# Layer 2 of a four-layer convolution kernel: raw v instead of a normalised copy, output statistics as sums on ScalarE, taps shared anew, and three pieces of work placed elsewhere

## The chip, the cores and the metric

The kernel runs on one core of a Trainium2 chip. The metric is the device time of one execution in microseconds (us); the time of a kernel is the median of its runs. Engines are named as the profile names them: PE is TensorE (PEld its weight loads), DVE is VectorE, ACT is ScalarE, POOL is GpSimd, and SP is the engine whose queue issues most transfers.

## The reference

Eight images of 128 channels and 96 x 96 points, in float32, go through four layers. Each adds to its input a convolution of its group normalisation (32 groups of four channels):

```
for layer in (L0, L1, L2, L3):
    x = x + conv_layer(group_norm_32(x))

L0: deformable 3x3 convolution (DCNv4): depthwise 3x3, layer norm, gelu, then
    offsets and masks per point, bilinear samples, weighted sum
L1: dense 3x3 convolution, 128 -> 128 channels
L2: q  = sign(x);  xq = (q - tanh(alpha_x * x)) + tanh(alpha_x * x)
    wq = the same of weight and alpha_w
    out = dwconv3x3(xq, weight) + dwconv3x3(x, wq)
L3: row by row over H: row h adds to row h+1 a relu of a 9-tap convolution along W, with bias
```

In L2 the `x` of the formulas is already normalised: x = sc * v + bi, where v is the output of layer 1 and sc, bi are one number per image and channel.

## The kernel before

The 128 channels are the 128 partitions. The kernel has three stages.

*Layer 0* ends at about 3472 us of the span. Its samples are taken as weighted sums over 25 shifts, which holds while no offset exceeds 1. Each chunk adds what exceeds 1 into a column of `beyond`; after the last chunk these are reduced to one number, `flag`, which all engines read (`values_load`, then `tc.If`) to choose between the fast way and a fallback.

*Layers 1 and 2* are one stage, from 3477 to 4828 us; its tiles have names that end in C. An image is cut into 12 chunks of 8 rows (`NCH` = 12, `CR` = 8).

- `conv_chunk(i, c)` does layer 1 for one chunk: it loads y with one row more on either side (`yw`), normalises it on ACT (L1252), forms four combinations `d` on POOL (L1259), multiplies them on PE with weights of 128 x 128 (L1272), and adds the four products on DVE into `vn` (L1288, L1296, L1308). `bn_stats` on DVE (L1317) collects the statistics of v. Two whole images of v are kept, `vns[i % 2]`, each with a border of one point.
- `v_coefs(i)` turns the statistics of an image into `sc_v`, `bi_v` (bn_aggr, two small PE products with a matrix of group means, one square root on ACT).
- An ACT pass (L1546), one operation for each chunk, then overwrites v with its normalised value. The border stays zero.
- `tap_chunk(i, c)` does layer 2 for one chunk. ACT makes sign and tanh (`sg` L1355, `th` L1357), POOL makes of them `xq` (L1362, L1368). There are 17 taps and a centre: eight of v with weights `wsg`, nine of `xq` with weights `w2s`. The centre of v is an ACT operation into PSUM (L1444). A tap can go one of three ways. POOL's way: ACT makes a scaled copy `pt` (L1414) and POOL adds such copies up (L1423). PE's way: eight products with diagonal matrices of 64 x 64 (`dgv` for v, `dgx` for xq, L1385), which PE adds up in PSUM. DVE's way: one multiply-and-add on PSUM (L1406). PE then merges the sums of POOL and of DVE (after a copy `ac` on ACT, L1458) into its own (L1392). ACT evicts the result to `o` (L1467), SP stores it, and two `bn_stats` on DVE (L1480) take the statistics of the output.
- `out_coefs(i)` turns these into `sc3`, `bi3`, the scale and offset of layer 3.

How many taps go which way is in two tables, `TAPS1` for images 0 to 6 and `TAPS2` for the last one: pairs (POOL, PE) for chunk 0, 1, 2, 3, then again; DVE has the rest of the 17.

Taps run `LAG` = 14 chunks behind the convolution, so that image i's convolution runs beside image i-1's taps. Each engine executes in the order in which the instructions were written. That order comes from the class `Plan`: every piece of work is a `task` with an engine, an assumed cost, what it depends on, a priority and the buffers that it uses. `Plan.order` walks through time with these costs and gives each free engine the ready task of lowest priority number whose buffers are free. For PE, a task of the same tile shape (64 or 128 wide) is preferred while its priority is within `KEEP` of the best. The constants at the top of the file (`PE_AT`, `DVE_AT`, `SUM_AT`, ...) shift priorities.

*Layer 3* runs from 4828 to the end; its names end in D. `load(g)` brings four rows of all eight images into `xtD` (1.5 MB), with three such groups resident. `norm(g, i)` (L1634) makes the normalised copy `xgD` on ACT. Then for each row DVE prepares (`row`, L1656 and L1658; `tr`, L1660 to L1662), PE multiplies (L1675), ACT applies the relu (L1614) and POOL adds it to the next row (L1615). Loads 0 and 1 are issued on POOL's queue after everything of layer 2; the SBUF of layer 2's tiles is taken over by layer 3's. `late_weights` prepares layer 3's weights: one load, `k3s`, and six DVE operations, `km` (L1159 to L1164), at the start of the stage of layers 1 and 2.

Of the kernel before, what the change touches and what calls it, by code (L numbers as in the profile page):

```python
# [19 lines left out]
P = 128  # L20
NG = 8
GC = P // NG
K2 = 9
# [8 lines left out]
TAPS1 = ((4, 6), (4, 5), (3, 6), (4, 6))  # L32
TAPS2 = ((3, 11), (1, 10), (5, 10))


POOL_AT, MERGE_AT = -22, 13
PE_AT, PE_PACE = 5, 5.3
DVE_AT, DVE_PACE = -57, 1.4
L1_AT, L1_PACE = -4, 0.0
SUM_AT = 2  # L40
STATS_AT = 59
KEEP12 = 14.0
# [171 lines left out]
def kernel(  # L214
# [197 lines left out]
    with ExitStack() as ph:  # L412
# [310 lines left out]
        def chunk(i, c, at, made):  # L723
# [37 lines left out]
            for k in (1, 0):  # L761
# [29 lines left out]
                plan.task(  # L791
# [5 lines left out]
                )  # L797
# [137 lines left out]
        squares = {}  # L935
        weights = conv_weights(-STEP * NST)
        made = {0: image(0, -STEP * NST)}
        for i in range(N):
            for c in range(NST):
                at = STEP * (i * NST + c)  # L940
                chunk(i, c, at, made[i])
            plan.task("DVE", 0.7, lambda i=i: y_stats(i), squares[i], at + 2 * STEP)
            if i + 1 < N:
                made[i + 1] = image(i + 1, STEP * i * NST)
        with tc.manual_schedule():
            plan.emit()


            m1 = sp.tile([P, 1], F32, name="m1")
            nc.vector.tensor_reduce(m1[:], beyond[:], AX.X, ALU.max)  # L950
            pt = plan.pools["s"].tiles[0]
            nc.tensor.transpose(pt[:1, 0, :P], m1[:], ident[:])
            m2 = sp.tile([1, 1], F32, name="m2")
            nc.vector.tensor_reduce(m2[:], pt[:1, 0, :P], AX.X, ALU.max)
            nc.vector.tensor_scalar(flag[:], m2[:], 0.0, None, ALU.is_gt)
# [137 lines left out]

    sc3 = const.tile([P, N], F32, name="sc3")
# [7 lines left out]
    with ExitStack() as ph:  # L1102
        wp = ph.enter_context(tc.tile_pool(name="wpC", bufs=1))
# [7 lines left out]
        for name, n, shape in (  # L1111
            ("yw", 3, [P, CR + 2, W + 2]), ("d", 2, [P, 4, NP1, W + 2]),
            ("sg", 2, [P, CR + 2, W]), ("th", 2, [P, CR + 2, W]), ("xq", 3, [P, CR + 2, W + 2]),
            ("ac", 2, [P, CB, FB]), ("o", 2, [P, NB, FB]), ("pt", 8, [P, CB, FB]),
        ):
            tiles = [wp.tile(shape, F32, name=f"{name}C{k}") for k in range(n)]
            if name in ("yw", "xq"):
                for t in tiles:
                    nc.gpsimd.memset(t[:, :, 0:1], 0.0)
                    nc.gpsimd.memset(t[:, :, W + 1 : W + 2], 0.0)  # L1120
            plan.pool(name, tiles)
# [8 lines left out]
        dgs = [wp.tile([P, K2, HC], F32, name=name) for name in ("dgv", "dgx")]  # L1130

        def tap_weights(at):


            def signs():
                nc.scalar.activation(wsg[:], w2s[:], AF.Sign)
                nc.scalar.activation(wth[:], w2s[:], AF.Tanh, scale=alw[:])

            def both():
                nc.vector.tensor_tensor(wsg[:], wsg[:], wth[:], ALU.subtract)  # L1140
                nc.vector.tensor_tensor(wsg[:], wsg[:], wth[:], ALU.add)

            def diagonal(dg, w, t):
                nc.vector.tensor_scalar(dg[:, t, :], idq[:], w[:, t : t + 1], None, ALU.mult)

            s = plan.task("ACT", 1.9, signs, [], at)
            s = plan.task("DVE", 0.4, both, [s], at)
            return [s] + [
                plan.task("DVE", 0.16, lambda a=(dg, w, t): diagonal(*a), [s], at)
                for dg, w in zip(dgs, (wsg, w2s)) for t in range(K2)  # L1150
            ]

        def late_weights(at):

            ld = plan.task("SP", 0.6, lambda: nc.sync.dma_start(k3s[:], k3), [], at, lag=4.0)
            v = nc.vector
            t = []
            for fn in (
# [12 lines left out]
                for name, n in (  # L1171
                    ("st2", NCH * CB * 6), ("st3", NB * NCH * 6), ("wc", 1),
                    *((f"{a}_{b}", 1) for a in ("mean", "v", "sd", "sc", "bi") for b in "yv"), ("mv_v", 2),
                    ("mv_o", 2 * NB), ("d_o", NB), ("mean_o", 1), ("sd_o", 1),
# [23 lines left out]
        def group_coefs(i, kind, mv, deps, prio):  # L1198
# [3 lines left out]

            def mid(ps):
                nc.vector.tensor_copy(mean[:], ps[:, 0, 0:1])
                add_square(v[:], ps, 0, mv[:, 0:1], mv[:, 1:2])

            b1 = plan.buf("v")
            t = plan.task(
                "PE", 0.4, lambda: nc.tensor.matmul(b1.tile[:, 0, 0:1], gmean[:], mv[:, 0:1], start=True, stop=True),
                deps, prio, uses=[b1],  # L1210
            )
# [113 lines left out]
        def v_coefs(i, stats, at):  # L1325
            s = smalls[i % 2]
            mean_y, sc, bi, sd, mv = s["mean_y"], s["sc_v"], s["bi_v"], s["sd_v"], s["mv_v"]

            def aggr():
                nc.vector.bn_aggr(mv[:], s["st2"][:])  # L1330
                nc.vector.tensor_scalar(mv[:, 0:1], mv[:, 0:1], mean_y[:], None, ALU.add)

            t = plan.task("DVE", 0.9, aggr, stats, at)
            t = group_coefs(i, "v", mv[:], [t], -1e6)

            def end():
                nc.vector.tensor_scalar(bi[:], mean_y[:], sc[:], bi[:], ALU.mult, ALU.add)

                nc.vector.tensor_scalar(s["wc"][:], sd[:], wsg[:, CENTER : CENTER + 1], None, ALU.add)

            return plan.task("DVE", 0.4, end, [t], -1e6)


        def tap_chunk(i, c, norms, at, n_pool, n_pe):
# [7 lines left out]
            near = norms[max(c - 1, 0) : c + 2]  # L1352

            readers = [
                plan.task("ACT", 1.0, lambda: nc.scalar.activation(sg.tile[:, :n, :], v, AF.Sign), near, at - 24, uses=[sg]),  # L1355
                plan.task(
                    "ACT", 1.05, lambda: nc.scalar.activation(th.tile[:, :n, :], v, AF.Tanh, scale=alx[:]), near, at - 23, uses=[th]  # L1357
# [23 lines left out]
            def tap_pe(src, t, first):  # L1381
                for j in range(NB):
                    for b in range(CB):
                        t_, rows, cols = source(src, t, b, RB)
                        nc.tensor.matmul(  # L1385
                            pq.tile[half(b), j, :FB], dgs[src][half(j), t, :], t_[half(j), rows, cols], start=first, stop=False
# [16 lines left out]
            def tap_dve(src, t):  # L1403
                w = (wsg, w2s)[src]
# [5 lines left out]
            for k, (_, t) in enumerate(all_taps[:n_pool]):  # L1410
# [4 lines left out]
                        rows_of(pt.tile[:]), rows8(0, t), AF.Identity, scale=wsg[:, t : t + 1]  # L1415
# [32 lines left out]
            for k, (src, t) in enumerate(all_taps[n_pool + n_pe :]):  # L1448
# [9 lines left out]
                lambda: nc.scalar.activation(ac.tile[:], pd.tile[:, :, :FB], AF.Identity, bias=s["mean_v"][:]),  # L1458
# [7 lines left out]
            t = plan.task(  # L1466
                "ACT", 0.82, lambda: nc.scalar.activation(o.tile[:], pq.tile[:, :, :FB], AF.Identity), [t], at + 10, uses=[pq, o]  # L1467
            )

            def store():  # L1470
# [7 lines left out]
            st = s["st3"][:].rearrange("p (j c k) -> p j c k", j=NB, k=6)  # L1478
            stats = [
                plan.task("DVE", 0.49, lambda j=j: nc.vector.bn_stats(st[:, j, c, :], o.tile[:, j, :]), [t], at + STATS_AT, uses=[o])  # L1480
                for j in range(NB)
            ]
            return readers, stats

        def out_coefs(i, stats, at):
# [3 lines left out]
            mv, d, mean, sd = s["mv_o"][:].rearrange("p (j k) -> p j k", k=2), s["d_o"], s["mean_o"], s["sd_o"]  # L1489
            st = s["st3"][:].rearrange("p (j f) -> p j f", j=NB)  # L1490

            def aggr():
                for j in range(NB):
                    nc.vector.bn_aggr(mv[:, j, :], st[:, j, :])

            def means(ps):
                nc.tensor.matmul(ps[:, 0, 0:NB], gmq[:], mv[:, :, 0], start=True, stop=True)
                for j in range(NB):
                    nc.tensor.matmul(ps[half(j), 1, 0:1], gmq[:, half(0)], mv[:, j, 0:1], start=True, stop=True)

            def mid(ps):
                nc.vector.tensor_copy(mean[:], ps[:, 1, 0:1])
                for j in range(NB):
                    add_square(d[:, j : j + 1], ps, j, mv[:, j, 0:1], mv[:, j, 1:2])
# [24 lines left out]
        weights = tap_weights(20 * 4)  # L1529
        late_weights(20 * 2 * NCH)  # L1530
        for i in range(N):
# [6 lines left out]
            done = v_coefs(i, stats + ends.get(i - 2, []) + (weights if i == 0 else []), 20 * (i + 1) * NCH)  # L1538
            made[i] = [done]
            norms = []  # L1540
            for c in range(NCH):
                s = smalls[i % 2]
                rows = inner(vns[i % 2], c * CR, (c + 1) * CR)
                norms.append(plan.task(
                    "ACT", 0.98,
                    lambda rows=rows, s=s: nc.scalar.activation(  # L1546
                        rows, rows, AF.Identity, bias=s["bi_v"][:], scale=s["sc_v"][:]
                    ),
                    [done], 20 * (i * NCH + c + LAG) - 45,
                ))  # L1550
            outs = []
            for c in range(NCH):
                taps = TAPS1 if i < N - 1 else TAPS2
                readers, st = tap_chunk(i, c, norms, 20 * (i * NCH + c + LAG), *taps[c % len(taps)])
# [11 lines left out]
    with ExitStack() as ph:  # L1566

        wp = ph.enter_context(tc.tile_pool(name="wpD", bufs=1))
        xts = [wp.tile([P, N, LG, W], F32, name=f"xtD{g}") for g in range(3)]
        xgs = [wp.tile([P, N, LG, W], F32, name=f"xgD{g}") for g in range(3)]  # L1570
# [68 lines left out]
        with tc.manual_schedule():  # L1639
            for g in range(2):  # L1640
                load(g, nc.gpsimd)
# [122 lines left out]
```

## Time and profile before

| What | us |
|---|---|
| median of three runs | 5604.98 (5604.57 to 5605.74) |
| the profiled execution, its own time | 5606.45 |
| its span in the profile | 5604.7 |
| busy: PE | 5382.2 (96% of the span) |
| busy: DVE | 4839.3 (86%) |
| busy: POOL | 4554.4 (81%) |
| busy: ACT | 3371.5 (60%) |

The granted clock is 0.99 over the span. Shares over the whole span are averages over three stages with different work. For this change the stage of layers 1 and 2, from 3477 to 4828 us, its beginning and its two ends matter; they are read by windows. An operation in the profile is named by line, engine, tile written and tile read.

### The profile page before, as it was taken

The numbers are of one execution on the slowest core, as the hardware profiler recorded it, in microseconds if no ns is written. First come the engines' busy times: TensorE is split into PE (matmuls) and PEld (weight loads), VectorE is DVE, ScalarE is ACT, GpSimd is POOL, SyncE is SP. The second block draws the span as 40 slices with busy tenths as digits, with TensorE's granted clock in tenths as the row PEclk, the third lists the DMA queues.
The fourth block names the chain that finished last, engine by engine and source line by source line (L and its number), as shares of the span: only waits on it lengthen the run. The fifth ranks groups of instructions, "written<-read, shape, count | busy, mean of one in ns | idle before, by whom it ended". The sixth has DMA issues, their size and how long they took to land. (4 is left out here: it accounts for less than half of the span.)

```text
span 5604.7 us, 128829 instructions
## 1 busy us (share of the span) xinstructions
PE 5382.2 (96%) x53049; PEld 3007.8 (54%) x53049; DVE 4839.3 (86%) x6874; ACT 3371.5 (60%) x4816; POOL 4554.4 (81%) x2835
## 2 busy tenths in 40 slices
PE   5899999999999999999999998999999999899999
PEld 2354454454454454454454443545454554699999
DVE  5788888888888888888888998699999998688887
ACT  4656666656766666666666663477787777533333
POOL 0899999999999999999999998699999998422222
PEclk9999999999999999999999999999999999999999
DMA  6121121221212112112111111222222221223232
GB/s 128 48 60 58 54 61 58 56 61 58 56 59 60 54 58 61 55 59 60 46 49 47 43 41 40 61 67 64 66 67 67 65 66 48 83 95 109 94 110 80
DMA packets 423809, 360.65 MB, mean 64 GB/s; under 512 B 251889, under 2 KB 422417, under 8 KB 423217
## 3 DMA queue, kind: packets, MB, share of 16 engines
q1 hardware_dynamic: 390336, 310.33, 19.7%
q10 hardware_dynamic: 32144, 38.87, 2.0%
q8 instruction: 422, 6.91, 0.5%
q0 software_dynamic: 736, 3.15, 0.2%
q14 instruction: 171, 1.39, 0.1%
HBM read 201.26 MB, written 150.99 MB: 63 GB/s over the span
## 5 line engine op out<-in xcount | busy, mean ns | idle before, releaser
L862 PE MATMUL ps_w<-wt,sel 64*64 64x384 f32 x19200 | 1857.1, 488 | 58.7 <-DVE h L809 17.2
L879 DVE TENSOR_TENSOR pr<-ps_w,xq 128x768 f32<-128x768 f32 x1824 | 1670.0, 949 | 209.4 <-PE ps_w L862 158.7
L852 POOL TENSOR_TENSOR wt<-h,h 128x768 f32<-128x768 f32 x864 | 1583.9, 1838 | 262.1 <-DVE h L809 140.3
L897 POOL TENSOR_TENSOR acc<-acc,pr 128x768 f32<-128x768 f32 x882 | 1618.6, 1837 | 72.4 <-DVE pr L879 60.0
L862 PEld LDWEIGHTS ps_w<-wt,sel 64*64 64x64 f32 x19200 | 743.9, 133 | 925.3 <-issue 287.7
L1272 PE MATMUL pv_C<-dC,km 128*128 128x384 f32 x2304 | 776.2, 491 | 11.9 <-POOL dC L1259 5.0
L839 PE MATMUL ps_s<-pr,idq 64*64 64x384 f32 x7536 | 761.6, 484 | 1.7 <-DVE pr L879 1.1
L1406 DVE SCALAR_TENSOR_TENSOR ps_C<-xqC,w2s,ps_C 128x768 f32<-128x768 f32 x674 | 683.8, 1015 | 85.7 <-ACT ps_C L1444 70.9
L767 ACT ACTIVATE o<-ps_w,omb 128x768 f32<-128x768 f32 x192 | 172.7, 899 | 810.9 <-PE ps_w L748 705.8
L1615 POOL TENSOR_TENSOR xtD<-xtD,cr 128x384 f32<-128x384 f32 x192 | 192.0, 1000 | 575.2 <-ACT cr L1614 513.2
L628 PE MATMUL ps_w<-xq,dwd 64*64 64x384 f32 x6624 | 631.3, 487 | 13.3 <-ACT x L648 6.9
L1272 PEld LDWEIGHTS pv_C<-dC,km 128*128 128x128 f32 x2304 | 426.1, 189 | 359.1 <-issue 47.3
L879 DVE TENSOR_TENSOR ps_w<-ps_w,xq 128x768 f32<-128x768 f32 x480 | 459.9, 958 | 94.7 <-PE ps_w L862 93.5
L757 ACT ACTIVATE h<-o,shift 128x768 f32<-128x768 f32 x576 | 533.1, 926 | 11.1
L780 ACT ACTIVATE h<-h 128x768 f32<-128x768 f32 x576 | 485.8, 843 | 17.4
L1423 POOL TENSOR_TENSOR ptC<-ptC,ptC 128x768 f32<-128x768 f32 x255 | 476.6, 1869 | 1.1
L839 PEld LDWEIGHTS ps_s<-pr,idq 64*64 64x64 f32 x7536 | 307.3, 133 | 302.7 <-issue 164.3
L886 DVE TENSOR_TENSOR acc<-ps_w,acc 128x768 f32<-128x768 f32 x480 | 456.1, 950 | 6.7
L748 PE MATMUL ps_w<-x1c,omq 64*64 64x384 f32 x4608 | 434.7, 490 | 18.3 <-DVE pr L879 14.9
L628 PEld LDWEIGHTS ps_w<-xq,dwd 64*64 64x64 f32 x6624 | 279.1, 133 | 278.0 <-issue 122.0
L1675 PE MATMUL ps_b<-tr,km 128*128 128x192 f32 x2304 | 407.5, 325 | 16.5 <-DVE tr L1660 16.5
L1675 PE MATMUL ps_a<-tr,km 128*128 128x192 f32 x2304 | 406.2, 324 | 0.0
(198 smaller groups left out, 7165.0 us busy)
## 6 DMA issues: line engine op xcount, KB each, us to landing
ywC<-y SPq DMA_DIRECT2D x80, 480.0 KB, 3.9
acc<-in_x SPq DMA_DIRECT2D x192, 192.0 KB, 3.4
x1c<-x1d SPq DMA_DIRECT2D x192, 192.0 KB, 3.3
y<-y SPq DMA_DIRECT2D x96, 384.0 KB, 3.3
x<-oC SPq DMA_DIRECT2D x192, 192.0 KB, 2.8
out<-xtD ACTq DMA_DIRECT2D x24, 1536.0 KB, 5.7
x1d<-x SPq DMA_DIRECT2D x92, 384.0 KB, 2.8
xtD<-x SPq DMA_DIRECT2D x22, 1536.0 KB, 7.0
```

What stands on the lines that cost most here:

```text
L628: nc.tensor.matmul(ps.tile[half(j), b, :FB], dwd[half(b), j, t, :], xq[half(b), r0 : r0 + RB, j, c0 : c0 + W], start=(t == 0), stop=(t == ...
L757: nc.scalar.activation(h, o, AF.Abs, bias=shift[:, k * NR + r : k * NR + r + 1])
L780: lambda h=h: nc.scalar.activation(h.tile[:], h.tile[:], AF.Relu, bias=1.0, scale=-1.0),
L839: nc.tensor.matmul(total.tile[half(j), b, :FB], idq[half(b), :], pr.tile[half(b), j, :], start=first, stop=last)
L852: lambda wt=wt, hy=hy, hx=hx: nc.gpsimd.tensor_tensor(wt.tile[:], hy.tile[:], hx.tile[:], ALU.mult),
L862: nc.tensor.matmul(ps.tile[half(b), j, :FB], sel[half(j), n, :], wt.tile[half(j), b, :], start=True, stop=True)
L879: nc.vector.tensor_tensor(view(pr.tile), view(ps.tile), x_s, ALU.mult)
L897: lambda pr=pr, acc2=acc2: nc.gpsimd.tensor_tensor(acc2.tile[:], acc2.tile[:], pr.tile[:], ALU.add),
L1272: nc.tensor.matmul(flat(ps), km1[:, k, x_, :], d.tile[:, k, :, x_ : x_ + W], start=(x_ == 0), stop=(x_ == 2))
L1406: nc.vector.scalar_tensor_tensor(view, rows8(src, t), w[:, t : t + 1], view, ALU.mult, ALU.add)
L1423: lambda a=parts[0], b=pt: nc.gpsimd.tensor_tensor(a.tile[:], a.tile[:], b.tile[:], ALU.add),
L1675: nc.tensor.matmul(ps[:, at_f : at_f + nf], km[:, k, t, :], tr[:, par, :, v : v + HW2], start=(t == 0), stop=(t == NT - 1),)
```

## The change

- Layer 2 reads v as it is. The pass L1546 goes. Sign and tanh take scale and offset in their ACT operation; the weights of the taps of v are multiplied by `sc` for each image (`wv`), with nine new diagonals in one of two sets (`dgv0`, `dgv1`). The border of v gets the value that normalises to zero (`edges`: four small ACT operations for each image). The constant that is left is in `bias`.
- The output is evicted in two halves, each with a running sum (`accum_out`), and two ACT squares with such a sum, about a centre `nmv`, take the place of two `bn_stats`. `means` makes `nmv` with four more small PE products for each image. `aggr` becomes eight small DVE operations.
- The tables `TAPS1`, `TAPS2` and the constants of the order are others. The mean number of taps for a chunk on POOL, PE and DVE goes from 3.75, 5.75, 7.5 to 3.75, 5.25, 8.0 in `TAPS1`, and from 3, 10.33, 3.67 to 2, 10.75, 4.25 in `TAPS2`.
- The flag's reductions are tasks of layer 0's plan. The taps' weights come after chunk 3 of the first image, layer 3's weights after image 2's coefficients.
- `yw`, `d`, `sg` and `th` get a pool of SBUF of their own (`wx`), which layer 3's `xtD0`, `xgD0` and `xtD1` take over. In the written order, load 0 then follows the last chunk's `xq` on POOL's queue; load 1 stands on SP's queue ahead of the last four chunks' stores; seven of the eight norms of group 0 stand on ACT ahead of the evictions of the last three chunks.

```diff
-TAPS1 = ((4, 6), (4, 5), (3, 6), (4, 6))
-TAPS2 = ((3, 11), (1, 10), (5, 10))
+TAPS1 = ((4, 5), (4, 6), (3, 5), (4, 5))
+TAPS2 = ((3, 11), (1, 11), (1, 10), (3, 11))
-POOL_AT, MERGE_AT = -22, 13
-PE_AT, PE_PACE = 5, 5.3
-DVE_AT, DVE_PACE = -57, 1.4
-L1_AT, L1_PACE = -4, 0.0
-SUM_AT = 2
+POOL_AT, MERGE_AT = -22, 14
+PE_AT, PE_PACE = -2, 5.1
+DVE_AT, DVE_PACE = -67, -0.0
+L1_AT, L1_PACE = -6, 0.2
+SUM_AT = -13
-KEEP12 = 14.0
+KEEP12 = 2.0
...
+        t = plan.task("DVE", 0.35, lambda: nc.vector.tensor_reduce(m1[:], beyond[:], AX.X, ALU.max), checks, -1e6)
+        t = plan.task("PE", 0.4, lambda: nc.tensor.transpose(pt.tile[:1, 0, :P], m1[:], ident[:]), [t], -1e6, uses=[pt], lag=0.1)
+        plan.task("DVE", 0.45, set_flag, [t], -1e6, uses=[pt])
         with tc.manual_schedule():
             plan.emit()
-            nc.vector.tensor_reduce(m1[:], beyond[:], AX.X, ALU.max)
-            nc.tensor.transpose(pt[:1, 0, :P], m1[:], ident[:])
-            nc.vector.tensor_reduce(m2[:], pt[:1, 0, :P], AX.X, ALU.max)
-            nc.vector.tensor_scalar(flag[:], m2[:], 0.0, None, ALU.is_gt)
...
+            pool = wx if name in ("yw", "d", "sg", "th") else wp
...
+                if kind == "v":
+                    for j in range(NB):
+                        for b in range(NB):
+                            nc.tensor.matmul(ps[half(b), 0, 1 + j : 2 + j], gmean[:, half(j)], mv[:, 0:1], start=True, stop=True)
...
+                v.tensor_scalar(s["edge"][:], s["mean_v"][:], mean_y[:], None, ALU.subtract)
+                v.tensor_scalar(s["wv"][:], wsg[:], sc[:], None, ALU.mult)
+                v.tensor_scalar(s["wc"][:], s["wv"][:, CENTER : CENTER + 1], 1.0, None, ALU.add)
+                v.tensor_scalar(s["bias"][:], wsum[:], bi[:], mean_y[:], ALU.mult, ALU.add)
+                v.tensor_scalar(s["th_sc"][:], alx[:], sc[:], None, ALU.mult)
+                v.tensor_scalar(s["th_bi"][:], alx[:], bi[:], None, ALU.mult)
+            def edges():
+                for part in (vn[:, 0, :], vn[:, H + 1, :], vn[:, 1 : H + 1, 0:1], vn[:, 1 : H + 1, W + 1 : W + 2]):
+                    nc.scalar.activation(part, part, AF.Identity, bias=s["edge"][:], scale=0.0)
...
-                plan.task("ACT", 1.0, lambda: nc.scalar.activation(sg.tile[:, :n, :], v, AF.Sign), near, at - 24, uses=[sg]),
+                plan.task("ACT", 1.0, lambda: nc.scalar.activation(sg.tile[:, :n, :], v, AF.Sign, bias=s["bi_v"][:], scale=s["sc_v"][:]), near, at - 24, uses=[sg]),
...
-            t = plan.task(
-                "ACT", 0.82, lambda: nc.scalar.activation(o.tile[:], pq.tile[:, :, :FB], AF.Identity), [t], at + 10, uses=[pq, o]
-            )
+            def evict():
+                for j in range(NB):
+                    nc.scalar.activation(o.tile[:, j, :], pq.tile[:, j, :FB], AF.Identity, accum_out=st[:, 0, j, c : c + 1])
+            def squares():
+                for j in range(NB):
+                    nc.scalar.activation(
+                        ac.tile[:, j, :], o.tile[:, j, :], AF.Square, bias=s["nmv"][:, j : j + 1], accum_out=st[:, 1, j, c : c + 1]
+                    )
...
-            stats = [
-                plan.task("DVE", 0.49, lambda j=j: nc.vector.bn_stats(st[:, j, c, :], o.tile[:, j, :]), [t], at + STATS_AT, uses=[o])
-                for j in range(NB)
-            ]
+            stats = [plan.task("ACT", 1.4, squares, [t], at + STATS_AT, uses=[o, ac])]
...
-        weights = tap_weights(20 * 4)
-        late_weights(20 * 2 * NCH)
+            weights = tap_weights(20 * 6, stats[CB * 3 : CB * 4]) if i == 0 else []
+            if i == min(2, N - 1):
+                late_weights(20 * (i + 1) * NCH + 40, made[i])
-            for c in range(NCH):
-                norms.append(plan.task(
-                    "ACT", 0.98, lambda rows=rows, s=s: nc.scalar.activation(rows, rows, AF.Identity, bias=s["bi_v"][:], scale=s["sc_v"][:]),
-                    [done], 20 * (i * NCH + c + LAG) - 45,
-                ))
...
-        xts = [wp.tile([P, N, LG, W], F32, name=f"xtD{g}") for g in range(3)]
-        xgs = [wp.tile([P, N, LG, W], F32, name=f"xgD{g}") for g in range(3)]
+        xts, xgs = [wx.tile(size, F32, name="xtD0")], [wx.tile(size, F32, name="xgD0")]
+        xts.append(wx.tile(size, F32, name="xtD1"))
...
-            for g in range(2):
-                load(g, nc.gpsimd)
+            load(0, nc.gpsimd)
+            load(1)
```

## The prediction

> **What bounds the kernel now.** I read the windows first: one for the start of the stage of layers 1 and 2, one for each image in its middle, one for its end, one for layer 3. The columns are span, then busy time and count of PE, PEld (weight load), DVE, ACT and POOL, then clock and DMA.
>
> ```profile
> 3492.60:3587.00 94.40, 93.87 (x292) 55.00 (x293) 51.75 (x90) 14.10 (x12) 46.59 (x51) 1.00 0.25 62
> 4228.00:4390.20 162.20, 160.87 (x1052) 81.57 (x1051) 147.89 (x226) 123.02 (x138) 154.83 (x109) 1.00 0.26 66
> 4710.50:4828.60 118.10, 106.13 (x1272) 49.14 (x1264) 72.97 (x106) 102.62 (x119) 96.10 (x50) 0.97 0.19 48
> 4828.60:4845.00 16.40, 1.34 (x4) 1.37 (x5) 2.42 (x7) 4.89 (x8) 1.93 (x2) 0.50 0.83 289
> 4845.00:5604.70 759.70, 750.42 (x4605) 750.13 (x4604) 626.93 (x1340) 252.45 (x568) 191.95 (x192) 0.99 0.28 94
> ```
>
> With one image in convolution and the one before it in taps (second row), PE is busy 160.9 of 162.2 us, POOL 154.8, DVE 147.9, and ACT has 39 us free. Layer 3 is PE as well. Between the two, PE does 1.3 us in 16.4.
>
> Then the waits of that second window (engine, waiting line, releaser: us in all, times, longest):
>
> ```profile
> ACT oC L1467 <- PE ps_C L1392: 10.7, 8, 4.0
> DVE vn L1288 <- PE pv_C L1272: 5.6, 6, 1.6
> POOL sgC L1362 <- ACT thC L1357: 6.0, 1, 6.0
> PE ps_C L1385 <- ACT oC L1467: 0.9, 1, 0.9
> ```
>
> The others wait for PE, and PE waits for nearly nothing. POOL has one hole of 6.0 us, at the boundary of two images, where the norms of v must precede its sign and tanh.
>
> The chain of waits shows the two places where PE isn't the limit: the start of the stage, and the step into layer 3 (start, us, what).
>
> ```profile
> 3480.41 6.01 DMA k3s<-in_k
> 3486.44 0.55 DVE km L1159
> ...
> 3491.95 0.53 DVE vn L1288
> 3492.49 0.14 issue
> 3492.62 7.66 PE pv_C L1272 x23
> ```
>
> ```profile
> 4822.11 0.82 ACT oC L1467
> 4822.95 1.02 DVE st3C L1480 x2
> 4823.97 0.73 DVE mv_oC L1494 x2
> 4827.74 0.22 DVE bi L329
> 4828.64 11.18 DMA xtD<-x
> 4840.05 2.51 ACT xgD L1634 x4
> 4843.66 4.18 PE ps_b L1675 x12
> ```
>
> At the start, VectorE's six operations on layer 3's weights stand ahead of the sums that release PE. At the end, layer 3's first load is issued only after the last coefficient.
>
> **Part by part.** *Flag.* Its reductions go into the last chunk's stream. They end at 3472.0 now; the image statistics that must end anyway end at 3470.74. So −1.3, at most −2.5 if the jump's 4.85 us also starts earlier; −1.4.
>
> *Weights of layer 3.* Load and six operations go behind image 2's coefficients. PE's first 12 products run from 3483.91 and would be done, at 0.323 us each (93.1 us for 288), at 3487.8; what follows starts at 3492.62. So −4.8, or −3 if ScalarE's norms of y then come late. At their new place they cost DVE 5.5 us once, in an image with 14 us free, and nobody needs the result before layer 3. The taps' signs and diagonals, now after chunk 3 of the first convolution, lie there beside DVE's 51.8 and ACT's 14.1 of 94.4 us (first row): nothing; without that cover, nine diagonals and the signs, some 5 us.
>
> *Middle images.* A tap or merge on PE is eight 64-wide products, 0.645 us. Per image the shares drop PE's units from 93 to 87: −3.87. Counting changes between 128-wide and 64-wide products in PE's written order gives 30 per image now, 26 after. The first group after a change is longer (1.45 for 16 products against 1.29): 4 × 0.178 = −0.71. Four small matmuls for the group means come in: their rows are 0.21 to 0.26 long and overlap, so about 0.14 each, +0.55. Sum −4.0, from 161.7 to 157.7.
>
> What must fit beside that: POOL keeps 3.75 taps per chunk, so 154.8. DVE loses 24 statistics × 0.548 = 13.2 and gains six taps × 1.015, nine diagonals of 0.3 and small ones: about 145. ACT loses 12 norms × 1.02 = 12.2 and gains, per chunk, a second half of the eviction and two squares. The nearest rows: the 384-wide relu of layer 3 takes 0.516, and reading an accumulator 0.19. So 2 × 0.71 in place of 0.81, and 2 × 0.71 more: +2.0 per chunk, 24.3 per image; with four edge strips about 136 of 158. That fits on average, and POOL's hole may shrink since no norms stand there. But POOL would run at 98%, so I take 158.2: −3.5 an image. Seven images: −24.5. The last image has 177 units for 172: +3.2. Net −21.3; bounds −26 (nothing lost) and −8 (half of the gain).
>
> A rule speaks against moving the statistics. The Trainium skill's "ScalarE: Activation LUTs", section "Rules for kernel authors", sends adds and multiplies to VectorE, not ScalarE. Its timing (186 ns plus 0.833 per column, 93 more for a bias pointer) would give estimates of 0.51 and 0.60 for the two forms; the rule's sum would be a loss of work, 24 us for 13. The rows say that the 24 come out of idle time, and the 13 don't; I go by the rows.
>
> *Last image begins* (4713 to 4757, PE idle 8.5 in pieces). Without norms sign and tanh start sooner, but diagonals are rebuilt first (9 × 0.3): −1, from −3 to +1.
>
> *Into layer 3.* Two loads go ahead of the end; the first stands on POOL's queue behind the last xq (L1368), the second on SP's ahead of the last four chunks' stores. If it has landed by then, the way from the last coefficient to PE shrinks from 4827.96–4843.66 (15.7) to the memsets, the copy of a row (0.37) and the first tr (0.60), about 2.2: −13.5. The statistics' chain gets longer: split eviction +0.4, squares for bn_stats +0.35, eight small operations (0.2 each) for two aggregations +1.05: +1.8. And a new wait: seven of the eight norms of the first group stand in ScalarE's order ahead of the evictions of chunks 9, 10 and 11, and wait for that load. Queued behind them are these evictions, and behind chunk 9's, PE's taps of chunk 11, which need its PSUM bank. Count from PE's last merge of chunk 7: last tanh at +3.2, two POOL passes (2.2 each) to +7.5, load +11.2 (its duration now, three loads in flight) to +18.7, seven norms × 0.61 to +23.0, eviction to +24.3; now chunk 11 starts at +18.7. So +5.6, bounds 0 (chunk 8's work covers a short load) and +8 (the load shares the queues with the stores). The SP load in front of stores delays them alone; the o buffers, two, are freed by these: at worst in the +8. Net −13.5 + 1.8 + 5.6 = −6, from −12 to −3.
>
> For the transfer there is a page: "DMA: Bandwidth & Descriptors", section "Anatomy of one DMA — SWDGE (gpsimd) path", fits 2.0 us plus bytes over 436,000 per us. By that estimate 1.57 MB lands in 5.6 us, ScalarE waits for nothing, and the step into layer 3 would be worth −12; the row's 11.18 was taken with three loads at once.
>
> Sum: −1.4 − 4.8 − 21.3 − 1 − 6 = −34.5. The profiled execution took 5606.45 (span 5604.7, 1.75 around it), so 5572 there; it was 1.5 over the median of the runs, so **5570**.
>
> **Rivals.**
>
> *POOL is the bound behind PE.* Its 154.8 busy and the 6.0 hole make 160.8, and PE's lower load then only waits. For: POOL's work isn't reduced, and in the changed order some 3 us more of it stand ahead of the first subtraction of an image. Against: the hole is a wait for tanh, which comes sooner without norms. The images then keep 161 (−0.7 × 7), and the last image's +3.2 stays: −1.4 − 4.8 − 1.7 − 1 − 6 = −15, 5590.
>
> *Slower: ScalarE's queue.* Squares and second halves are short but in order; where one stands before the centre tap, ac or a POOL tap's copy that is due, PE's next merge comes later. Over 84 chunks of the middle images −34.5 is used up at 0.41 us each; the added work is 2.0 per chunk. At a third of it exposed, 0.66: +55 − 34.5, 5625. Against: ACT has 39 us free of 162, and eviction waits 10.7 for PE, not PE for it.
>
> *The first load is the end.* The wait for it eats the tail (+8 and slow stores): inside the range at −28, 5577. That the edits do not act at all can be excluded for the flag and weights, since the written order of the instructions has them moved; if the load, too, were still late, −29 instead of −34.5.
>
> **How the numbers follow.** A measurement can tell about 0.2%, 11 us. My forecast, 5553 to 5584: 0.62. POOL as the bound, 5584 to 5599: 0.20. Its worse form, with a third of ScalarE's price on top, 5594 to 5616: 0.08. ScalarE's queue, beyond 5616: 0.10. So faster 0.82, the same 0.08, slower 0.10. The range 5553 to 5599 holds the first two.
>
> **What would show it.** Right: middle images of about 158 with PE still at 99%, ACT 136, POOL's hole under 4 us; PE's run of products starting within 1 us after the first twelve; from the last coefficient to PE about 2 us; a wait of ScalarE for the DMA into xtD at the end, with PE idle some 5 us in chunk 11. Wrong: an image at 161 with PE waiting for xq or the POOL taps (first rival); PE waiting for ACT ac or eviction in every chunk (second); DVE over 152; squares longer than 0.8.

## The result, and the profile after

The changed kernel takes 5683.61 us (median; 5677.64 to 5685.11), the kernel before 5604.77 beside it: 1.0143 of it, interval 1.0131 to 1.0156. The forecast was 5570, with 5553 to 5599 as range. The time went the other way, by 79 us.

The windows after, for a middle image, the last image's taps, the step into layer 3, and layer 3 (columns as before):

```profile
4432.30:4603.30 171.00, 158.95 (x1018) 81.06 (x1014) 160.85 (x229) 133.21 (x216) 155.54 (x111) 0.96 0.24 63
4773.70:4919.30 145.60, 123.33 (x1416) 56.15 (x1408) 87.50 (x132) 116.89 (x222) 81.56 (x43) 0.93 0.23 66
4919.30:4921.60 2.30, 0.05 (x1) 0.08 (x1) 1.92 (x7) 0.71 (x1) 0.00 (x0) 0.50 0.42 53
4921.60:5682.20 760.60, 751.41 (x4608) 751.12 (x4608) 628.42 (x1342) 252.54 (x568) 192.57 (x192) 0.99 0.28 96
```

PE has less to do per middle image, as forecast, but the image lasts 171 us instead of 162: PE is idle for 12 of them. DVE, forecast at 145 us, is busy 160.9. The step into layer 3 shrank as forecast, layer 3 is unchanged, and the taps of the last image are 21 us longer.

The groups of DVE's operations in that stage (count, then busy us, mean ns) show where its time went:

```profile
L1529 DVE TENSOR_SCALAR mv_oC<-e_oC 128x4 f32<-128x4 f32 x8 | 64.2, 8023 | 0.3
L1141 DVE TENSOR_SCALAR dgv<-idq,wvC 128x64 f32<-128x64 f32 x72 | 27.2, 455 | 0.0
L1355 DVE TENSOR_SCALAR wvC<-wsg,sc_vC 128x9 f32<-128x9 f32 x8 | 16.1, 2013 | 0.0
L1167 DVE TENSOR_TENSOR km<-k3s 128x384 f32<-128x384 f32 x1 | 6.9, 6873 | 0.0
L1532 DVE TENSOR_SCALAR e_oC<-mv_oC,nmvC 128x1 f32<-128x1 f32 x16 | 3.3, 209 | 0.3
L1220 DVE TENSOR_SCALAR nmvC<-pv_C 128x2 f32<-128x2 f32 x8 | 1.2, 149 | 0.0
```

L1529 divides four sums by the number of points. It has four elements per partition and takes 8 us on average, 16.1 at most; the last one, after all GpSimd work of this stage, takes 0.17. Its neighbour L1532, with one element, takes 0.21. The wait lies inside the operation, so the list of waits puts it down to no releaser. DVE, PE and GpSimd (POOL) around one of them, from the timeline:

```profile
4482.36 0.20 DVE L1528 TENSOR_REDUCE e_oC<-st3C 128x4 f32<-128x48 f32 x1
4482.60 12.27 DVE L1529 TENSOR_SCALAR mv_oC<-e_oC 128x4 f32<-128x4 f32 x1
4494.91 0.21 DVE L1532 TENSOR_SCALAR e_oC<-mv_oC,nmvC 128x1 f32<-128x1 f32 x1
```

```profile
4494.93 0.58 PE L1537 MATMUL pv_C<-mv_oC,gmq 128*128 128x2 f32 x2 [11.14 <-DVE mv_oC L1529]
```

```profile
4483.29 2.27 POOL L1395 TENSOR_TENSOR xqC<-sgC,thC 128x960 f32<-128x960 f32 x1
4485.46 1.86 POOL L1450 TENSOR_TENSOR ptC<-ptC,ptC 128x768 f32<-128x768 f32 x1
4487.23 2.26 POOL L1389 TENSOR_TENSOR sgC<-sgC,thC 128x960 f32<-128x960 f32 x1
4489.39 1.85 POOL L1450 TENSOR_TENSOR ptC<-ptC,ptC 128x768 f32<-128x768 f32 x1
4491.15 3.70 POOL L1272 TENSOR_TENSOR dC<-ywC 128x392 f32<-128x392 f32 x4
4497.48 2.21 POOL L1395 TENSOR_TENSOR xqC<-sgC,thC 128x960 f32<-128x960 f32 x1 [2.63 <-issue]
```

L1529 starts at 4482.60 and ends at 4494.87; GpSimd's unbroken run ends at 4494.85. All seven long ones end 0.02 to 0.03 us after the end of a GpSimd operation. Five of them (9.1 to 16.1 us) lasted over six to ten ends of GpSimd operations, until GpSimd itself stood still for 2.6 to 8.2 us. The other two (1.18 and 2.08 us) ended with the GpSimd operation in progress, though the next one followed at once. What let VectorE in there isn't shown. Behind L1529 stand DVE's sums and taps; on PE the small product L1537 stands at the head of the queue and waits 11.14 us, with all products behind it. Over the whole stage TensorE's queue waited there for L1529 52.4 us, in six places.

Two pages of the Trainium skill bear on this. "GPSIMD Engine Reference", section "Specifications", says that GpSimd's access to SBUF is shared with VectorE, with contention from VectorE instructions in a two-port mode or with two inputs in SBUF. "VectorE: DVE Perf Modes", section "What auto-detection actually checks", gives the two-port mode to an operation with one source when source and destination are in SBUF and their outermost dimensions that are not 1 are both even or equal. The rows agree: 128x4, 128x64 and 128x9 wait, 128x1 and the one with its source in PSUM (L1220) don't, and L1167, with two sources in SBUF, does. How long the wait lasts is read from the rows above.

### The profile page after: what moved, and what is told of

Its sections match the earlier page's. It is cut to its first block, busy times and chain, and to the rows that moved or that the text cites. A ratio compares the mean times of both kernels' runs of the same rounds, so it can differ in the third digit from the quotient of the medians.

```text
span 5682.2 us, 128778 instructions
## 1 busy us (share of the span) xinstructions
PE 5382.1 (95%) x52817; PEld 3010.4 (53%) x52817; DVE 4937.4 (87%) x6891; ACT 3444.9 (61%) x5414; POOL 4529.9 (80%) x2822
## 5 line engine op out<-in xcount | busy, mean ns | idle before, releaser
L1433 DVE SCALAR_TENSOR_TENSOR ps_C<-xqC,w2s,ps_C 128x768 f32<-128x768 f32 x723 | 735.5, 1017 | 72.2 <-ACT ps_C L1471 61.3
L1450 POOL TENSOR_TENSOR ptC<-ptC,ptC 128x768 f32<-128x768 f32 x243 | 444.1, 1828 | 2.6 <-ACT ptC L1441 2.2
L1272 POOL TENSOR_TENSOR dC<-ywC 128x392 f32<-128x392 f32 x384 | 357.9, 958 | 110.8 <-PE pv_C L1285 68.5
```

Of the source, the lines that this page charges most:

```text
L1433: nc.vector.scalar_tensor_tensor(view, rows8(src, t), w[:, t : t + 1], view, ALU.mult, ALU.add)
```

## The experiments

Theory A is that wait. Theory B: VectorE waits there for its own input. Theory C: ScalarE's order, the slower rival of the prediction. The runs of the kernel before beside each experiment had medians of 5600.7 to 5603.3; since these differ a little from chip to chip, kernels are compared by their ratio to it.

**Scale by ones.**

```diff
-  nc.vector.tensor_scalar(mv, e, 1.0 / (NCH * FB), None, ALU.mult)
+  for k in range(2):
+      for j in range(NB):
+          nc.vector.tensor_scalar(mv[:, k, j:j+1], e[:, k, j:j+1], 1.0 / (NCH * FB), None, ALU.mult)
```

> The changed kernel, with the scaling of the sums (L1529: one VectorE operation on 128x4, 8.0 us on average, 16.1 at most, always ending where GpSimd's run of operations has a gap) written as four operations on 128x1 each. Theory A, that an operation on several SBUF elements with one source has to wait for a gap of GpSimd, while a one-element operation doesn't (L1532 to L1534 right behind it take 0.21 each): the four take 0.2 each, TensorE's waits of 60 us at the means (L1537) go, and the time falls by 45 to 65 us from 5683.6, to 5619 to 5639. Theory B, that VectorE waits there for its own preceding reduction or for ScalarE's sums: the first of the four takes as long as the one, time 5675 to 5685. Theory C, that the loss is ScalarE's order (two eviction halves and squares): the operation becomes short, but the time falls by less than 15 us.

Measured: 5619.73, ratio 1.0032 (1.0018 to 1.0046). From the groups of this kernel:

```profile
L1531 DVE TENSOR_SCALAR mv_oC<-e_oC 128x1 f32<-128x1 f32 x32 | 2.7, 147 | 0.3
```

Four operations in place of one take 0.15 us each, and 64 us are gone. A is borne out, B falls (the input is the same), C can't be the main loss.

**The same operation put into the kernel before**, in three forms between the aggregation and the means:

```diff
-  nc.vector.bn_aggr(mv[:, j, :], st[:, j, :])
+  nc.vector.bn_aggr(mw[:, j, :], st[:, j, :])
...
+  nc.vector.tensor_scalar(mv, mw, 1.0, None, ALU.mult)          # e4: one source, 128x4
+  nc.vector.tensor_tensor(mv, mw, mw, ALU.max)                  # e9: two sources, 128x4
+  nc.vector.tensor_scalar(mv[:, j, k:k+1], mw[:, j, k:k+1], ...)  # e13: four of 128x1
```

> The kernel before, with one operation added to each image's output coefficients: a VectorE scale by 1.0 on 128x4 between the aggregation and the means, like the one of the changed kernel. Theory A: it waits for gaps of GpSimd, 5 to 10 us in each of seven images, TensorE with it, and the time rises by 30 to 65 us from 5604.8. Theories B and C: eight times 0.17 us, no more than 3 us.

> The kernel before with the extra operation as a VectorE tensor-tensor maximum of the 128x4 with itself, two sources in SBUF, in place of the one-source scale. If two sources in SBUF wait for GpSimd as well (as the first km sum did, 6.9 us): 10 to 13 us each in six images and some 5675 us; if only the one-source form waits: 0.2 us each and 5605.

> The kernel before with the same extra scale by 1.0 as e4_before_with_scale, written as four operations on 128x1. Theory A: 0.15 to 0.21 each, no wait, 5604 to 5610. If anything put at this place of VectorE's order costs what e4 cost: some 5675.

Measured: e4 5678.84, ratio 1.0134 (1.0117 to 1.0151); e9 5679.85 in one run; e13 5600.86, ratio 1.0000 (0.9989 to 1.0010). The group of e4, then of e9, then of e13:

```profile
L1496 DVE TENSOR_SCALAR mv_oC<-mw_oC 128x4 f32<-128x4 f32 x8 | 74.0, 9247 | 0.3
```

```profile
L1496 DVE TENSOR_TENSOR mv_oC<-mw_oC 128x4 f32<-128x4 f32 x8 | 73.6, 9201 | 0.3
```

```profile
L1498 DVE TENSOR_SCALAR mv_oC<-mw_oC 128x1 f32<-128x1 f32 x32 | 3.0, 135 | 0.2
```

Eight operations without effect on the result make the kernel before 75 us slower, about as much as the whole change does (79); as 32 of one element they cost nothing that can be measured. The form with two sources waits as long.

**The same with less work on GpSimd.**

```diff
-TAPS1 = ((4, 6), (4, 5), (3, 6), (4, 6))
-TAPS2 = ((3, 11), (1, 10), (5, 10))
+TAPS1 = ((1, 6), (1, 6), (1, 6), (1, 6))
+TAPS2 = ((1, 11), (1, 10), (1, 10))
```

> As e4_before_with_scale (the kernel before with one VectorE scale on 128x4 per image), with GpSimd's share of the taps cut to one per chunk, so that it adds none (its taps go to VectorE; an image gets longer by VectorE's ten taps per chunk, so the whole time says nothing). Only the duration of the scale is asked. If it waits for a gap in GpSimd's run: GpSimd has four combinations and two passes, 8.2 us, per chunk of some 15 us, so that its runs are 2 to 8 us long, and the mean falls from 9.2 to 1 to 4 us, with the end of each wait still at the end of a GpSimd operation. If it waits for something else (its own input, memory, ScalarE): 9 us or more as before.

Measured, with GpSimd busy 104 of 190 us in the stretch from 3800 to 3990 us, and 89 to 93 us in images of 153 to 183 (5812.29 us in one run):

```profile
L1496 DVE TENSOR_SCALAR mv_oC<-mw_oC 128x4 f32<-128x4 f32 x8 | 3.8, 474 | 0.3
```

From 9247 ns to 474, below what I expected. Two of the eight didn't wait (0.17 us). The other six, of 0.22 to 0.91 us, ended 0.02 to 0.03 us after the end of the GpSimd operation in progress, four of them though the next one followed at once. So it is GpSimd that the operation waits for. A gap in GpSimd's work isn't needed to end the wait, but with less of that work the waits over many operations are gone.

**Weights and diagonals on ScalarE.** The two other places:

```diff
-  v.tensor_scalar(s["wv"][:], wsg[:], sc[:], None, ALU.mult)
+  nc.scalar.activation(s["wv"][:], wsg[:], AF.Identity, scale=sc[:])              # e2 and e5
-  nc.vector.tensor_scalar(dg[:, t, :], idq[:], w[:, t:t+1], None, ALU.mult)
+  nc.scalar.activation(dg[:, t, :], idq[:], AF.Identity, scale=w[:, t:t+1])       # e5
```

> As the run before, and the weights wv (L1355, 128x9 on VectorE, 2.0 us on average, up to 6.9) made by ScalarE instead. Theory A: another 5 to 15 us less than the run before, since these waits stand ahead of an image's diagonals and sign; the nine diagonals (128x64) then take the waiting instead in part. Theories B and C: within 5 us of the run before.

> The kernel of the third run (scale by ones, norm of image 7 first), with the weights wv and the nine diagonals of each image made by ScalarE. In the third run VectorE spent 31.9 us in the 72 diagonals, 17.9 at their shortest duration of 0.248, and 11.6 in the eight weights, 1.8 at their shortest. Theory A (these two wait for GpSimd's gaps too): 24 us of VectorE's waiting go, about 2.3 us an image come to ScalarE; time 6 to 15 us below that run's 5614.6. Rival (the waiting lay beside TensorE's own work, as in the second run, where the weights alone moved and nothing came of it): within 4 us.

The weights alone: 5625.58, ratio 1.0044 (1.0027 to 1.0061), no gain. The weights' 9.8 us on VectorE went, but the diagonals took the waiting over. Their rows in e1, then here:

```profile
L1141 DVE TENSOR_SCALAR dgv<-idq,wvC 128x64 f32<-128x64 f32 x72 | 32.3, 526 | 0.0
L1141 DVE TENSOR_SCALAR dgv<-idq,wvC 128x64 f32<-128x64 f32 x72 | 50.4, 1172 | 0.0
```

Both (on top of the next experiment's edit): 5583.23, ratio 0.9968 (0.9956 to 0.9979), 31 us below e3, where I had expected 6 to 15. That is more than the 24 us of waiting on DVE; how the rest comes about was not followed further. From here the change is a gain.

**The norms of layer 3's first group** behind the last coefficient (e3, on e1), and ahead again (e10, on e6):

```diff
-  for i in range(N):
+  for i in (N - 1, *range(N - 1)):
       norm(0, i)
```

> As the first run, and the norm of image 7 is put first among the eight of layer 3's first group, so that all of them stand on ScalarE behind the last coefficient and none ahead of the evictions of chunks 9 to 11. If ScalarE's wait for the first load (7.9 us) and the seven norms (4.3 us) hold TensorE's last chunk: TensorE's hole at the end goes (some 12 us), TensorE starts layer 3 some 3 us later behind the coefficients, net 6 to 9 us less than the first run. If the hole has another cause (GpSimd's last xq, the stores): no gain, up to 3 us more.

> As e6_km_in_image0, with the norms of layer 3's first group in the changed kernel's own sequence (image 0 first), so that seven of them stand on ScalarE ahead of the evictions of chunks 9 to 11 and wait for the load. If that wait holds TensorE's last chunk: a wait of ScalarE for the DMA of 5 to 12 us, the part from image 7's aggregation to layer 3's first product 5 to 9 us longer, time 5 to 9 us above e6's 5577. If it lies beside work: within 3 us, or 2.5 less, since the norms no longer stand between the last coefficient and layer 3.

Measured: e3 5614.60, ratio 1.0023 (1.0014 to 1.0033), 5 us below e1, whose runs scatter from 5607 to 5629, so that the two aren't told apart; e10 5584.80, ratio 0.9970 (0.9960 to 0.9979), 7.7 us above e6. From the waits of e10 in its last image:

```profile
PE ps_C L1421 <- ACT oC L1506: 12.3, 4, 8.5
ACT xgD L1679 <- DMA xtD<-x: 8.8, 1, 8.8
```

ScalarE waits 8.8 us for the load, and PE for the eviction behind it 8.5 at once. The wait forecast in the prediction is real: from the last aggregation of v to the last coefficient e10 takes 145.7 us, e6 135.2. In e6 the norms stand between that coefficient and layer 3 instead, where they cost 2.2.

**Layer 3's weights beside image 0** (e6, on e5):

```diff
-  if i == min(2, N - 1):
-      late_weights(20 * (i + 1) * NCH + 40, made[i])
+  if i == 0:
+      late_weights(20 * 7, stats[CB * 5 : CB * 6])
```

> As e5_weights_diagonals_on_act, and layer 3's weights (load k3s and the six km operations) are made beside the convolution of image 0, where GpSimd is busy 44.6 of 94.4 us, instead of beside image 3's, where the first sum of two SBUF tiles took 6.9 us and the third operation 2.1 for 0.55, and that image 180 us where its neighbours took 160 to 164. Theory A: the sums take 0.55 each and the time falls by another 8 to 18 us. Rival (image 3 is long for another reason): less than 3 us either way.

Measured: 5577.12, ratio 0.9954 (0.9937 to 0.9970). The sums take 0.55 to 0.56 each, and the time falls by 6 us, less than expected. This version beats both kernels. Its windows, two middle images, the last image's taps, and the part of these in which ScalarE is full:

```profile
4202.90:4361.10 158.20, 157.03 (x1018) 80.39 (x1014) 146.74 (x221) 135.44 (x226) 152.37 (x109) 1.00 0.26 68
4361.10:4519.30 158.20, 157.03 (x1018) 80.47 (x1014) 146.59 (x222) 135.89 (x226) 157.50 (x112) 1.00 0.26 68
4677.75:4812.90 135.15, 118.82 (x1404) 53.78 (x1396) 83.53 (x127) 114.11 (x221) 82.52 (x43) 0.95 0.25 71
4690.00:4735.00 45.00, 35.47 (x394) 15.29 (x390) 31.35 (x47) 42.73 (x72) 32.56 (x18) 0.89 0.15 39
```

With the waits gone a middle image takes 158.2 us, with PE at 99%, ACT at 135.

**The old tables, and the old statistics** (each on e6):

```diff
-TAPS1 = ((4, 5), (4, 6), (3, 5), (4, 5))                 # e8
+TAPS1 = ((4, 6), (4, 5), (3, 6), (4, 6))
...
-stats = [plan.task("ACT", 1.4, squares, [t], at + STATS_AT, uses=[o, ac])]    # e11
+stats = [plan.task("DVE", 0.49, lambda j=j: nc.vector.bn_stats(st[:, j, c, :], o.tile[:, j, :]), ...) for j in range(NB)]
```

> As e6_km_in_image0 with the two tables of shares as before (TensorE 93 tap and merge units per middle image, VectorE six taps fewer). If TensorE is what bounds a middle image once the waits are gone: 6 x 0.645 more in seven images and 5 x 0.645 less in the last, 20 to 25 us slower than e6_km_in_image0. If VectorE or ScalarE bounds it: within 6 us or faster.

> As e6_km_in_image0, with the output's statistics as before: one eviction, two bn_stats on VectorE per chunk, two aggregations. VectorE gets 24 x 0.548 = 13.2 us more per middle image, ScalarE about 24 less. If the move to ScalarE is what makes room for VectorE's half tap more per chunk: VectorE comes to some 154 of 158 us, its order gets too tight, and the time rises by 5 to 20 us. If VectorE has room anyway: within 4 us. If ScalarE's order is what costs (the second rival of the prediction): faster by more than 4.

Measured: e8 5603.56, ratio 1.0003 (0.9994 to 1.0013), 26 us above e6; TensorE's units have about the price that the prediction gave them. e11 5632.45, ratio 1.0054 (1.0037 to 1.0071), 55 us above e6, far over the 5 to 20 expected. Two stretches of 166 us of e11, one image each:

```profile
4220.00:4386.00 166.00, 162.92 (x1011) 77.26 (x1011) 155.07 (x236) 119.98 (x140) 154.94 (x110) 1.00 0.25 64
4386.00:4552.00 166.00, 163.28 (x998) 77.27 (x1002) 153.95 (x234) 120.05 (x140) 153.66 (x109) 0.99 0.25 64
```

DVE is at the 154 to 155 forecast, and PE is busy 163 us with about as many products that took 157 in e6: the planned order is another one too, and these runs don't part its share from VectorE's. Theory C asked for a faster run here, so it falls: with these shares of taps the move of the statistics to ScalarE is a gain.

## Why the prediction was wrong

The parts, from the traces, in us (before to after, and before to e6, the version without the waits; the limits are the last square of layer 0, the aggregations of v, the last coefficient, layer 3's first product):

| Part | predicted | after | e6 |
|---|---|---|---|
| start of the stage, image 0 | −6.2 | −5.1 | −5.7 |
| image 1 | −3.5 | −8.3 | −6.2 |
| images 2 to 7 | −21.0 | +86.3 | −14.8 |
| last image's taps to the last coefficient | +9.6 | +21.5 | +11.0 |
| step into layer 3 | −13.5 | −13.6 | −11.4 |
| layer 3 itself | 0 | −0.4 | +0.1 |

Layer 0 ended 2.8 us earlier in the profiled run after and 0.7 later in e6's; with that the columns add up to the differences of the spans, +77.5 and −26.3.

- *The step that failed is the price of the small VectorE operations.* "Eight small operations (0.2 each)", "nine diagonals of 0.3 and small ones: about 145", and layer 3's weights that "cost DVE 5.5 us once": L1529 took 8.0 on average, a weight operation 2.0, one km sum 6.9. I took durations from places where GpSimd was idle or one element was written, and carried them to places where GpSimd hardly pauses. In the middle images I counted them as VectorE's load alone: that TensorE stands at the means' products until L1529 ends had no term, and it was 52.4 us. L1529 written as ones brought 64 us of the 114 between forecast and measurement; weights and diagonals on ScalarE brought 31 (part of it unexplained), layer 3's weights beside image 0 brought 6.
- *The profile of before held two hints.* In layer 0, `y_stats` divides two sums by the number of points as L1529 divides four, again from SBUF to SBUF (shortest, median and longest duration in ns):

```profile
L930 DVE TENSOR_SCALAR ymv<-yd x8: 168/1190/3919, 589.9 to 3469.8; 128x2 f32<-128x2 f32 x8
```

The shortest is the last one, with GpSimd idle; the seven others started beside a GpSimd operation and took 0.73 us and more. A look at this row would have put a wait into the price of L1529. And the six km operations, at the stage's start, took 0.55 for the first and the last, but 1.26 and 1.23 for two sums of the same 128x384, which took 0.56 and 0.55 in e6. The same form with different durations points to a wait inside the operation. I put the sum of 5.5 us into the account and didn't ask why it wasn't 3.3.
- *The rivals.* The first one (GpSimd as the bound) named the right engine for the wrong reason: its load isn't what bounds; VectorE's wait behind its operations is. The second (ScalarE's queue) had the right sign and fell with e11.
- *PE's terms were right.* Six units fewer in a middle image: 158.2 us forecast, 158.2 measured in e6; the old tables put 26 us back for 20 to 25 expected. Images 2 to 4 of e6 took 161.1, 158.5 and 160.0, so that the sum for the images is smaller than forecast.
- *The start* came as forecast within about 1 us, *the step into layer 3* exactly: 2.1 us from last coefficient to first product.
- *The wait for layer 3's first load* was forecast at +5.6 with bounds 0 and 8; it showed as 7.9 us of ScalarE's waiting after, 8.8 in e10. With the norms behind it, it made the way to the last coefficient 10.5 us longer in e10 than in e6, over the upper bound of 8; the step into layer 3 is 2.2 shorter there, and the medians differ by 7.7. The load took 12.37 from issue to landing after and 10.7 in e10, near the row of 11.18 I went by, and not near the 5.6 us estimated from the Trainium skill's "DMA: Bandwidth & Descriptors", section "Anatomy of one DMA — SWDGE (gpsimd) path".
- *The last image's taps* are 11.0 us longer in e6 even without that wait, for +4.0 forecast (3.2 − 1 + 1.8). In the 45 us of the window above, ACT is busy 42.7 and PE 35.5. I had averaged ACT over the whole part, where it has room, and not over the stretch in which sign, tanh, diagonals and squares of several chunks come together. The longest wait of PE in that stretch is one for ACT:

```profile
PE ps_C L1428 <- ACT acC L1494: 7.1, 1, 7.1
```

No run tests this, so that ScalarE is the cause of the 7 us stays an argument.
- *The sum.* e6's 5577 lies in the range partly by luck, since e6 lacks the wait for the load that the forecast counts at 5.6. With the changed kernel's own order of the norms (e10) it is 5585, 18 us below the kernel before where 34.5 were forecast: the images gave less than forecast, the last image's end cost more.

## What to carry to other kernels

A short VectorE operation on several SBUF elements may not be short beside a GpSimd that hardly pauses: before adding one, look for the same form in the profile where GpSimd is busy. If it waits there, write it in single elements (e1, e13), take its source from PSUM (L1220), or give it to ScalarE (e5). When one form of operation shows several durations in a profile, the longer ones may hold a wait that the list of waits doesn't show. Fix such a wait at all its places at once: with one place mended, the next such operation took the waiting over.

## What was not expected of the hardware

An operation of 0.17 us took up to 16.1 us while GpSimd's run lasted, and 0.47 on average where GpSimd was busy for about half the time (89 to 93 us of images of 153 to 183). VectorE's taps and sums, which work on PSUM, ran beside GpSimd without such waits (1017 ns per tap after, 1015 before), and so did `bn_stats`, `bn_aggr` and the reduction from SBUF (548 to 553 ns, 440 to 800 for the two sizes of aggregation, and 198). One form with a single source in SBUF didn't wait either: the copy that begins layer 3's weights (L1166, 128x384) took 537 ns with GpSimd busy throughout, so the number of elements alone doesn't decide.
